# Two half-width score products, an earlier load of c, and a reordered end of layer 0 in a two-layer AdaLN kernel

## The chip, the cores and the metric

The kernel runs on one core of a Trainium2 chip. The core has a tensor engine (PE) with its own path for loading weights (PEld), a vector engine (DVE), a scalar engine (ACT), a general-purpose engine (POOL) and a sync engine (SP) that issues DMA transfers. Each engine works through its own queue in order and waits on semaphores for the others. The metric is the device time of one execution in microseconds (us); the median of three runs before the change is 2544.6 us (2543.75 to 2546.12).

## What is computed

Two transformer layers with adaptive layer norm, on x of 2 batches x 512 positions x 512 features, all in float32. Cut to what matters here:

```python
mod = (silu(L0_c) @ L0_wmod).reshape(2, 6, 1, -1)      # sa, ca, ga, sb, cb, gb
h = layernorm(x) * (1 + ca) + sa
# layer 0 attention: 32 query heads, 8 key/value heads, head size 128, window of 128
q, k, v = rope(h @ wq), rope(h @ wk), h @ wv
scores = q @ k.T * HEAD_DIM ** -0.5
allowed = (j <= i) & (j > i - 128)
x = x + ga * (softmax(where(allowed, scores, -inf)) @ v) @ wo
h = layernorm(x) * (1 + cb) + sb
# layer 0 feed-forward: one 512x512 product, a bias and 16 low-rank updates
x = x + gb * (h @ W.T + bias + sum_e coeffs[e] * scales[e] * (h @ A[e].T) @ Bf[e].T)
# layer 1: the same frame round latent attention with 128 heads and a routed low-rank FFN
```

The limit to ga and gb in size and the whole of layer 1 are left out; the change does not touch them.

## The kernel before

**Tiles.** A position block is 128 rows; each batch has TB = 4 of them. In layer 0 the attention is divided into 16 units, a unit being one key/value head (a "group" of 4 query heads) of one batch: units 0 and 1 are group 0 of batch 0 and 1, and so on. A unit has four blocks of queries, qb = 0 to 3. Because of the window of 128, a block of queries sees its own block of keys and the one before: 256 columns of scores, or 128 for qb = 0. A wide tile of scores is thus 128 queries x 4 heads x 256 keys (two PSUM banks), a narrow one 128 x 4 x 128.

**Steps.** `attention0` writes out the order of PE, DVE, ACT and POOL by hand (`manual_schedule`); SP is not in that order. It runs steps n = -4 to 65. With u, qb = divmod(n, 4), a step issues, in this order: `scores` of (u, qb); the keys, values or queries of the next unit (one `queries` a step, with `keys` at qb = 0 and `values` at qb = 1); `normalised` (the division by the row sum); `turned` of step n - 1 (transposes of the probabilities, `pt`, copied to `pT` by ACT for the first half of the keys and by DVE for the second); `output` of step n - 2 (`pw`, four products with wo, and the addition to x); `mix` of step n - 1 (`po`, the products with v, copied to `oT` by DVE); one item of `aside` while there are any (the modulation rows for later use, `psr` and what follows); and the extra items of `steps`. What is in `rest` follows after the last step. Since no unit follows unit 15, steps 60 to 63 have no keys, values or queries.

**Scores.** `scores` (L598) issues four products, one for each head, of 128 queries x nk keys, then on DVE the addition of the mask `band` (L610) and the negated row maximum `nm` (L616), then on ACT four exponentials with row sums (L620). The tile `s` is allocated anew in each step from a pool with one buffer. `band` is one 128 x 256 table with 0 where a query sees a key and -1e30 elsewhere.

**The start.** `silu_c` (L78) loads c of each layer (4 KB) through POOL's queue; ACT's exponential and DVE's three small operations (L84, L85, L88) make `sc`, the stationary operand of the modulation products `psr` (L103). SP loads the first two 1 MB pieces of wmod, the eight blocks of x, the rotary table, band, and the weights of group 0. SP may have eight loads open, and a later one waits for the landing of an earlier one. `Norm` computes the statistics of a block (`stats`, L171 and L172 on DVE), then for a batch the root on ACT and the normalised rows `xn` on DVE (`rows`, L179 to L184), then 16 transposes `pst` and the scaled, shifted copies `hT`, shared by ACT and DVE (`turn`). This part is ordered by the scheduler.

**The end of layer 0.** `finale` places the feed-forward's first parts among the last steps. `end` is 56, the first step of unit 14:

```python
for i in range(TB):
    steps[end + 2 + i] = [lambda i=i: n0.stats(i)]
    steps[end + 6 + i] = [lambda i=i: n0.stats(TB + i)]
steps[end + 4].insert(0, f.bias)
steps[end + 5].append(lambda: n0.rows(0))
steps[end + 6].insert(0, lambda: n0.turn(0, (0, 1), pool))
```

Block i of batch 0 gets its last addition in `output` of step end + 2 + i, the step at whose end its statistics stand; `rows(0)` (root and xn) stands at the end of step 61, the turning of batch 0 at the ends of 62 and 63, the low-rank products `low` (`psxa`) at the ends of 63 and 64. `tile(t)` is the feed-forward of one block (`psf`), and `add_bias` adds the gated bias to x. `f.bias` also loads the bias row, into a buffer of the attention's pool. The products named here (`pw`, `po`, `pst`, `psxa`, `psf`) share four PSUM buffers in rotation.

Of the kernel before, what the change touches and what calls it, by code (L numbers as in the profile page):

```python
# [25 lines left out]
NKV, GRP, HD, WIN = 8, 4, 128, 128  # L26

# [15 lines left out]
def adaln_kernel(ctx: ExitStack, tc: tile.TileContext, A: dict, out: bass.AP):  # L43
# [34 lines left out]
    def silu_c(L, pool):  # L78

        c = pool.tile([P, KC, B], F32, tag=f"c{L}", name=f"c{L}")  # L80
        nc.gpsimd.dma_start(out=c, in_=A[f"L{L}_cT"])
        e = pool.tile([P, KC, B], F32, tag=f"ce{L}", name=f"ce{L}")
        nc.scalar.activation(e, c, AF.Exp, scale=-1.0)
        nc.vector.tensor_scalar_add(e, e, 1.0)  # L84
        nc.vector.reciprocal(e, e)  # L85
        sc = pool.tile([P, KC, 32], F32, tag=f"sc{L}", name=f"sc{L}")
        nc.gpsimd.memset(sc, 0.0)
        nc.vector.tensor_mul(sc[:, :, :B], c, e)  # L88
        return sc
# [126 lines left out]
    class Ffn0:  # L216
# [6 lines left out]
        def loads(self):  # L223
# [13 lines left out]
            for i, n in enumerate(("L0_ffn_coeffs", "L0_ffn_scales")):  # L237
                for j in range(2):
                    src = A[n][j * 8 : (j + 1) * 8].unsqueeze(1).to_broadcast([8, R]).unsqueeze(2)
                    nc.sync.dma_start(out=co[:, i, j : j + 1], in_=src)  # L240
            self.wrow = self.mid.tile([P, 2], F32, tag="wrow", name="wrow0")
            nc.vector.tensor_mul(self.wrow, co[:, 0, :], co[:, 1, :])

        def bias(self):

            row = self.ap.tile([P, D], F32, tag="t1", name="biasrow0")
            nc.sync.dma_start(out=row, in_=A["L0_ffn_bias"].unsqueeze(0).to_broadcast([P, D]))
# [3 lines left out]
            for b in range(B):  # L251
                nc.gpsimd.tensor_mul(self.gb[b], row, self.gate[b])
# [38 lines left out]
    with ExitStack() as c01:  # L291
# [7 lines left out]
        with ExitStack() as c00:  # L299
# [34 lines left out]
            def finale(ap, pool):  # L334
# [5 lines left out]
                for i in range(TB):  # L340
                    steps[end + 2 + i] = [lambda i=i: n0.stats(i)]
                    steps[end + 6 + i] = [lambda i=i: n0.stats(TB + i)]
                steps[end + 4].insert(0, f.bias)
                steps[end + 5].append(lambda: n0.rows(0))
                steps[end + 6].insert(0, lambda: n0.turn(0, (0, 1), pool))
                steps[end + 7] = [
                    lambda: n0.turn(0, (2, 3), pool), lambda: f.add_bias(0), lambda: f.low(0, 0)
                ] + steps[end + 7]
                steps[end + 8].insert(0, lambda: f.low(0, 1))
                rest = [  # L350
                    lambda: n0.rows(1),
                    lambda: f.tile(0),
                    lambda: f.tile(1),
                    lambda: n0.turn(1, range(KC), pool),
                    lambda: f.add_bias(1),
                    lambda: f.tile(2),
# [8 lines left out]
                return steps, rest  # L365
# [129 lines left out]
def weights0(tc, A, ctx):  # L495
# [10 lines left out]
    def tables():  # L506
# [3 lines left out]
        band = tab.tile([P, 2 * P], F32, tag="band", name="band")  # L510
# [18 lines left out]
def attention0(tc, small, hT, xs, ga, ident, tabs, groups, load_group, aside, finale):  # L529
# [11 lines left out]
    with ExitStack() as ctx:  # L541
# [4 lines left out]
        kTs, vs, qTs, oTs, sps, pes, pTs = ({} for _ in range(7))  # L546
# [51 lines left out]
        def scores(u, qb):  # L598

            k0, nk = window(qb)  # L600
            sp = pss.tile([P, GRP, 2 * P], F32, tag="s", name=f"s{u}_{qb}")
            for hh in range(GRP):
                nc.tensor.matmul(  # L603
                    sp[:, hh, :nk],
                    lhsT=qTs[u][:, hh, qb * P : (qb + 1) * P],
                    rhs=kTs[u][:, k0 * P : k0 * P + nk],
                    start=True,
                    stop=True,
                )
            nc.vector.tensor_add(  # L610
                sp[:, :, :nk],
                sp[:, :, :nk],
                band[:, 2 * P - nk :].unsqueeze(1).to_broadcast([P, GRP, nk]),
            )
            nm = small.tile([P, GRP], F32, tag="nm", name=f"nm{u}_{qb}")
            nc.vector.tensor_reduce(nm, sp[:, :, :nk], AX.X, ALU.max, negate=True)  # L616
            pe = ap.tile([P, GRP, 2 * P], F32, tag="p", name=f"p{u}_{qb}", bufs=3)
            rs = small.tile([P, GRP], F32, tag="rs", name=f"rs{u}_{qb}")
            for hh in range(GRP):
                nc.scalar.activation(  # L620
                    pe[:, hh, :nk], sp[:, hh, :nk], AF.Exp,
# [54 lines left out]
        steps, rest = finale(ap, pmm)  # L676
        aside.pop(0)()
        with tc.manual_schedule(engines=FOUR):
            for n in range(-TB, NU * TB + 2):
# [20 lines left out]
                if 0 <= n - 2:  # L700
                    output(*last)
                if 0 <= n - 1 < NU * TB:
# [546 lines left out]
def _constants():  # L1249
# [12 lines left out]
    band = np.where((j > i) & (j <= i + WIN), 0.0, -1e30).astype(np.float32)  # L1262
# [71 lines left out]
```

## Time and profile before

| what | us |
|---|---|
| median of 3 runs | 2544.6 |
| the profiled execution | 2545.36 |
| its span on the core | 2543.6 |
| PE busy | 2454.6 |
| POOL busy | 1592.2 |
| DVE busy | 1672.9 |
| ACT busy | 1400.6 |
| L603, scores of layer 0, wide, busy | 91.3 |
| L603, scores of layer 0, narrow, busy | 18.0 |
| PE waiting at psr (L103) for sc (L88) | 13.3 |
| PE waiting at po (L650) for pT (L641) | 8.2 |

The span runs from the first instruction to the last. Busy time of PE is the union of its records; one product of the program in float32 makes two records. A record's length reaches past the start of the next one, because products are pipelined, so the cost of a block of products is read from the distance between starts, not from the lengths. The form "128*64" in a line of PE is the part of the array used, rows x columns. The mean clock granted to PE in this execution was 0.979 of full speed.

### The profile page before, as it was taken

How to read it: one execution, taken by the hardware profiler on the slowest of the kernel's cores; microseconds unless marked ns; L12 is line 12 of the kernel's file. 1: busy time of each engine (PE TensorE's matmuls, PEld its weight loads, DVE VectorE, ACT ScalarE, POOL GpSimd, SP SyncE). 2: the span in 40 equal slices, each digit the busy share in tenths (PEclk: the TensorE clock that was granted, in tenths of full speed). 3: DMA queues.
4: the chain of work that ended last, by engine and by line, in shares of the span. 5: the costliest groups of instructions: out<-in, count | busy, mean ns of one | idle time of the engine just before them, and what ended most of it. 6: DMA issues, size and time to landing. Idle time of an engine off the chain costs nothing.

```text
span 2543.6 us, 28531 instructions
## 1 busy us (share of the span) xinstructions
PE 2454.6 (97%) x10268; PEld 1148.9 (45%) x10268; DVE 1672.9 (66%) x2323; ACT 1400.6 (55%) x2083; POOL 1592.2 (63%) x1538
## 2 busy tenths in 40 slices
PE   7999999999999999999999999999999999999757
PEld 3555555555555444444444344444444434444233
DVE  4545555555555345788777778777878777887652
ACT  2112212212112215888888788878888878888710
POOL 1333333333333314888888888888888888888841
PEclk9999999999999999999999999999999999999868
DMA  6211101001000101000000000000000000000010
GB/s 233 85 51 64 42 5 38 26 20 38 17 1 7 29 15 33 26 19 24 26 26 26 30 19 25 26 26 26 30 18 26 26 26 25 24 23 17 1 32 33
DMA packets 68477, 81.31 MB, mean 32 GB/s; under 512 B 6865, under 2 KB 49520, under 8 KB 68208
## 3 DMA queue, kind: packets, MB, share of 16 engines
q1 hardware_dynamic: 67984, 79.21, 9.8%
q8 instruction: 81, 1.33, 0.2%
q14 instruction: 60, 0.49, 0.1%
q0 software_dynamic: 352, 0.28, 0.1%
HBM read 77.38 MB, written 2.10 MB: 31 GB/s over the span
## 4 chain that ended last, share of the span: by engine, by line
PE 93%; issue 2%; DVE 2%; POOL 2%; ACT 1%; DMA 0%; SPq 0%; POOLq 0%; DVEq 0%; ACTq 0%
PE s L948 18%; PE psq L881 18%; PE acc L1103 9%; PE ps_q L552 9%; PE pw L664 8%; PE s L957 5%; PE s L603 4%; PE po L650 4%; PE psv L574 2%; PE ps_k L552 2%; PE pt L639 2%; PE psu L900 2%; PE psm L1027 1%; PE psw L1159 1%; PE psf L275 1%
## 5 line engine op out<-in xcount | busy, mean ns | idle before, releaser
L1054 POOL TENSOR_TENSOR ss<-ss,row 128x512 f32<-128x512 f32 x512 | 644.6, 1287 | 39.3 <-ACT row L1039 39.3
L967 ACT COPY ss<-s 128x1024 f32<-128x1024 f32 x512 | 505.6, 1015 | 167.4 <-PE s L957 128.8
L948 PE MATMUL s<-q,ckr 64*128 64x512 f32 x2048 | 552.9, 611 | 7.6 <-ACT ss L967 7.6
L1057 ACT ACTIVATE ss<-ss 128x1024 f32<-128x1024 f32 x512 | 525.7, 1070 | 8.4 <-POOL ss L1048 4.0
L881 PE MATMUL psq<-hT,wqr 128*128 128x512 f32 x1024 | 466.7, 598 | 0.0
L957 PE MATMUL s<-qm,c 64*128 64x512 f32 x1024 | 417.9, 794 | 0.0
L620 ACT ACTIVATE p<-s,nm 128x256 f32<-128x256 f32 (+1 forms) x256 | 111.1, 446 | 488.0 <-DVE nm L616 479.2
L974 DVE TENSOR_TENSOR mx<-s,mx 128x1024 f32<-128x1024 f32 x256 | 306.5, 1218 | 41.1 <-PE s L957 40.1
L562 POOL TENSOR_TENSOR qT<-t_q,t_q 128x512 f32<-128x512 f32 x64 | 81.3, 1270 | 402.4 <-DVE t_q L561 402.4
L1048 POOL TENSOR_TENSOR ss<-ss,rowe 128x512 f32<-128x512 f32 x256 | 323.3, 1286 | 0.0
L881 PEld LDWEIGHTS psq<-hT,wqr 128*128 128x128 f32 x1024 | 189.0, 189 | 242.3 <-issue 211.7
L948 PEld LDWEIGHTS s<-q,ckr 64*128 64x128 f32 x2048 | 183.4, 186 | 212.7 <-ACT ss L967 97.2
L1103 PE MATMUL acc<-ss,vp 128*32 128x512 f32 x2048 | 265.7, 607 | 5.5 <-ACT ss L1057 5.5
L974 DVE TENSOR_TENSOR mx<-s,ss 128x1024 f32<-128x1024 f32 x128 | 156.8, 1225 | 117.5 <-ACT row L1039 78.0
L664 PE MATMUL pw<-wo,oT 128*128 128x512 f32 x512 | 230.3, 592 | 0.0
L552 PE MATMUL ps_q<-hT,wq 128*128 128x512 f32 x512 | 230.1, 592 | 0.0
L979 DVE STREAM_TRANSPOSE mx<-mx 128x1024 f32<-128x1024 f32 x128 | 158.6, 1239 | 2.2
L985 DVE TENSOR_REDUCE m<-mx 128x32 f32<-128x1024 f32 x128 | 156.2, 1220 | 4.4
L1050 DVE TENSOR_TENSOR ss<-ss,psm 128x512 f32<-128x512 f32 x256 | 158.0, 679 | 0.0
L957 PEld LDWEIGHTS s<-qm,c 64*128 64x128 f32 x1024 | 104.2, 187 | 117.7 <-issue 114.8
L1017 POOL TENSOR_TENSOR st<-mh,own_block 128x512 fp32r<-128x512 f32 x64 | 67.1, 1048 | 139.0 <-DVE mh L1013 139.0
L552 PEld LDWEIGHTS ps_q<-hT,wq 128*128 128x128 f32 x512 | 96.0, 190 | 102.4 <-issue 100.8
(193 smaller groups left out, 3089.3 us busy)
## 6 DMA issues: line engine op xcount, KB each, us to landing
wqr<-in_L_attn_Wq_rope_pairs SPq DMA_DIRECT2D x64, 512.0 KB
wmod<-in_L_wmod SPq DMA_DIRECT2D x12, 1024.0 KB
wq<-in_L_attn_wq SPq DMA_DIRECT2D x8, 1024.0 KB
wo<-in_L_attn_wo SPq DMA_DIRECT2D x8, 1024.0 KB
x<-in_L_attn_x SPq DMA_DIRECT2D x8, 256.0 KB
wk<-in_L_attn_wk SPq DMA_DIRECT2D x8, 256.0 KB
wv<-in_L_attn_wv SPq DMA_DIRECT2D x8, 256.0 KB
wT<-in_L_ffn_WT SPq DMA_DIRECT2D x2, 1024.0 KB
```

Source lines behind the costliest of these rows:

```text
L552: nc.tensor.matmul(ps, lhsT=wcols(kc), rhs=hT[b][:, kc, :], start=(kc == 0), stop=(kc == KC - 1))
L664: nc.tensor.matmul(ps, lhsT=oTs[u][:, hh, i * P : (i + 1) * P], rhs=groups[g]["o"][:, hh, :], start=(hh == 0), stop=(hh == GRP - 1),)
L881: nc.tensor.matmul(ps, lhsT=wqs[t][:, kc, pair * P : (pair + 1) * P], rhs=hT[b][:, kc, :], start=(kc == 0), stop=(kc == KC - 1),)
L948: nc.tensor.matmul(out[:, j, :], lhsT=whole[b]["kr"][r, bass.ts(i, P)], rhs=qs[t, p][r, :], start=True, stop=False,)
L957: nc.tensor.matmul(out[:, j, :], lhsT=qkc[t // 2, 1][r, bass.ts(i, P)], rhs=qm[t, p][r, :], start=False, stop=True,)
L967: nc.scalar.copy(ss[t, i, p], hold["s", t, i, p])
L974: nc.vector.tensor_max(mx[t, p], hold["s", t, i, p], before)
L979: nc.vector.transpose(m, m)
L1048: nc.gpsimd.tensor_sub(s, s, hold["r", t, 2])
L1054: nc.gpsimd.tensor_sub(s, s, hold["r", t, 2 * p + 1])
L1057: nc.scalar.activation(ss[t, i, p], ss[t, i, p], AF.Exp)
L1103: nc.tensor.matmul(accs[g, b][32 * h : 32 * (h + 1), :], lhsT=vps[t][:, kb, h, :], rhs=ss[t, kb, h // 2][:, h % 2, :], start=(s == 0 and k ...
```

## The change

There are three parts.

1. **Scores of wide tiles.** The tile of scores is allocated once, and filled once with -1e30 by DVE. In a wide tile each head's product is replaced by two: the first 64 queries against keys 0 to 191 of the 256, the last 64 against keys 64 to 255. They write the two halves of the PSUM partitions. The corners that no product writes (queries 0 to 63 with keys 192 to 255, queries 64 to 127 with keys 0 to 63) are always masked: they keep the large negative value, and the mask has 0 there. The narrow tile now lies in the last 128 columns. `band` grows to 128 x 384, with the narrow mask in its last third. DVE and ACT work on the same number of elements as before.
2. **c.** Its two loads are issued by SP instead of POOL, and stand first in SP's queue.
3. **The end of layer 0.** The statistics of a block stand one step later, `rows(0)` at the end of step 62, the statistics of the last block in `rest`. The turning of batch 0 (all four), the bias addition and `low(0, 0)` go into step 63 between `output` and `mix`, `low(0, 1)` likewise into step 64 (`filling`). In `rest`, `tile(2)` is ahead of the turning of batch 1. The bias row is loaded with the feed-forward's other weights into a buffer of its own.

The order of SP, which the scheduler makes, changes in the place of these loads: the two c first, and coefficients and bias row behind the third pair of wmod pieces, where the coefficients stood ahead of it. At the start, DVE's order now has the six operations for `sc` ahead of all statistics, and the two copies of the modulation columns (`mod`, L122) between the first `xn` and the other three.

```diff
-        nc.gpsimd.dma_start(out=c, in_=A[f"L{L}_cT"])
+        nc.sync.dma_start(out=c, in_=A[f"L{L}_cT"])
...
+            self.row = self.mid.tile([P, D], F32, tag="biasrow", name="biasrow0")
+            nc.sync.dma_start(out=self.row, in_=A["L0_ffn_bias"].unsqueeze(0).to_broadcast([P, D]))
...
-            row = self.ap.tile([P, D], F32, tag="t1", name="biasrow0")
-            nc.sync.dma_start(out=row, in_=A["L0_ffn_bias"].unsqueeze(0).to_broadcast([P, D]))
...
                 for i in range(TB):
-                    steps[end + 2 + i] = [lambda i=i: n0.stats(i)]
-                    steps[end + 6 + i] = [lambda i=i: n0.stats(TB + i)]
+                    steps[end + 3 + i] = [lambda i=i: n0.stats(i)]
+                for i in range(TB - 1):
+                    steps.setdefault(end + 7 + i, []).append(lambda i=i: n0.stats(TB + i))
                 steps[end + 4].insert(0, f.bias)
-                steps[end + 5].append(lambda: n0.rows(0))
-                steps[end + 6].insert(0, lambda: n0.turn(0, (0, 1), pool))
-                steps[end + 7] = [
-                    lambda: n0.turn(0, (2, 3), pool), lambda: f.add_bias(0), lambda: f.low(0, 0)
-                ] + steps[end + 7]
-                steps[end + 8].insert(0, lambda: f.low(0, 1))
+                steps[end + 6].insert(1, lambda: n0.rows(0))
+
+                filling = {
+                    end + 7: [
+                        lambda: n0.turn(0, (0, 1), pool), lambda: n0.turn(0, (2, 3), pool),
+                        lambda: f.add_bias(0), lambda: f.low(0, 0),
+                    ],
+                    end + 8: [lambda: f.low(0, 1)],
+                }
                 rest = [
+                    lambda: n0.stats(NT - 1),
                     lambda: n0.rows(1),
                     lambda: f.tile(0),
                     lambda: f.tile(1),
+                    lambda: f.tile(2),
                     lambda: n0.turn(1, range(KC), pool),
                     lambda: f.add_bias(1),
-                    lambda: f.tile(2),
                     lambda: f.tile(3),
...
+        sp = pss.tile([P, GRP, 2 * P], F32, tag="s", name="scores")
+        nc.vector.memset(sp, NEVER)
...
             k0, nk = window(qb)
-            sp = pss.tile([P, GRP, 2 * P], F32, tag="s", name=f"s{u}_{qb}")
-            for hh in range(GRP):
-                nc.tensor.matmul(
-                    sp[:, hh, :nk],
-                    lhsT=qTs[u][:, hh, qb * P : (qb + 1) * P],
-                    rhs=kTs[u][:, k0 * P : k0 * P + nk],
+            o = 2 * P - nk
+            for hh in range(GRP) if qb == 0 else ():
+                nc.tensor.matmul(
+                    sp[:, hh, o:],
+                    lhsT=qTs[u][:, hh, :P],
+                    rhs=kTs[u][:, :P],
                     start=True,
                     stop=True,
                 )
+            for hh in range(GRP) if qb else ():
+                for h in range(2):
+                    lo, hi = h * H2, 2 * P - (1 - h) * H2
+                    nc.tensor.matmul(
+                        sp[h * H2 : (h + 1) * H2, hh, lo:hi],
+                        lhsT=qTs[u][:, hh, qb * P + h * H2 : qb * P + (h + 1) * H2],
+                        rhs=kTs[u][:, k0 * P + lo : k0 * P + hi],
+                        start=True,
+                        stop=True,
+                    )
...
                 if 0 <= n - 2:
                     output(*last)
+                for f in filling.get(n, ()):
+                    f()
                 if 0 <= n - 1 < NU * TB:
                     mix(*before)
...
+    band = np.concatenate([band, band[:, P:]], axis=1)
+    band[:H2, 2 * P - H2 : 2 * P] = 0.0
+    band[H2:, :H2] = 0.0
```

## The prediction, made before the changed kernel ran

> **What bounds the kernel now.** I read the page's busy shares and chain of waits first, then the busy time by stretches, to see where TensorE (PE) ever waits.
>
> ```profile
> PE 2454.6 (97%) x10268; PEld 1148.9 (45%) x10268; DVE 1672.9 (66%) x2323; ACT 1400.6 (55%) x2083; POOL 1592.2 (63%) x1538
> PE 93%; issue 2%; DVE 2%; POOL 2%; ACT 1%; DMA 0%; SPq 0%; POOLq 0%; DVEq 0%; ACTq 0%
> 60.00:810.00 750.00, 749.32 (x2708) 421.10 (x2707) 404.95 (x577) 151.66 (x559) 263.55 (x192) 1.00 0.10 33
> ```
>
> The last line is a stretch: its bounds and length, busy us (instructions) of PE, PEld (weight loads), DVE, ACT and POOL, then granted clock, DMA share, GB/s. PE carries 93% of the chain, and from 60 to 810 us, nearly all of layer 0's attention, it is busy for 749.3 of 750.0 us. In that stretch a microsecond taken from PE is a microsecond of the kernel, and work moved between the other engines is worth nothing. Before 60 us and from 810 to 868 us PE waits; there the waits decide.
>
> Next, PE's own timeline. Columns: start, length, engine, line, operation; the distance between two starts is what a block costs.
>
> ```profile
> 107.93 3.60 PE L552 MATMUL ps_q<-hT,wq 128*128 128x512 f32 x8
> 111.37 1.04 PE L639 MATMUL pt<-ident,p 128*128 128x128 f32 x8
> ...
> 115.68 1.88 PE L650 MATMUL po<-pT,v 128*128 128x512 f32 x4
> 117.49 3.63 PE L103 MATMUL psr<-wmod,sc 128*32 128x512 f32 x16
> 121.04 1.99 PE L603 MATMUL s<-kT,qT 128*128 128x256 f32 x8
> 122.88 3.73 PE L574 MATMUL psv<-wv,hT 128*128 128x128 f32 x32
> 391.40 1.89 PE L603 MATMUL s<-kT,qT 128*128 128x256 f32 x8
> 393.13 3.60 PE L552 MATMUL ps_q<-hT,wq 128*128 128x512 f32 x8
> 117.94 0.12 PEld L103 LDWEIGHTS psr<-wmod,sc 128*32 128x32 f32 x2 [0.31 <-issue]
> ```
>
> A product of the program makes two records. ps_q: 8 records in 3.44 us, 0.43 each. A wide score tile (L603): 8 records in 1.73 us, 0.216 each. psr is the one block here that already uses column parts of the array (128*32): 16 records in 3.55 us, so two run at once, at 0.43 a pair.
>
> **Scores on column halves.** Each of 48 wide tiles (16 units x 3) gives up 8 records of 256 columns and gets 16 of 64x192, in 8 pairs if the halves run together. A record's price follows its columns (512: 0.43, 256: 0.216), so 192 cost 0.162 and the tile 8 x 0.162 = 1.30 us instead of 1.73: 0.43 saved.
>
> Against it stands the change of array shape, which psr shows: po's four records should take 4 x 0.43 = 1.72 and psr starts after 1.81 (+0.09); psr should take 3.43 and lasts 3.55 (+0.12); the tile behind it lasts 1.84 instead of 1.73 (+0.11). Together 0.32 us. The 0.11 is the uncovered load of 128 columns, the first load of 32 columns is about 0.03 of the 0.12; 64 columns make that about 0.05. So one excursion costs 0.35 and a tile 1.65: **0.08 us saved**. Three wide tiles stand directly behind psr, where part of this is paid already (about 0.2 each).
>
> The Trainium skill has a rule against this ("TensorE: Matmul & The Clock Gate", Part 3, "The mechanism"): a weight load overlaps matmuls in flight only when its row group differs. Both halves use all 128 rows, so by the rule each pair would wait for its loads. psv shows loads at their limit: 32 of 128 columns in 3.57 us, 0.112 each, 0.056 for 64; 8 x 0.056 = 0.45 us a tile, 2.10 in all, 48 x 0.37 = 18 us *lost*. The row says otherwise: psr's loads run at 117.94, beside its matmuls, and its pairs keep ps_q's 0.43. I take the row. What it doesn't show is 64-column loads under a pair of only 0.162; a load record lasts 0.12 for 32 columns and 0.19 for 128, so I expect about 0.14, still covered, with little to spare.
>
> Sum: 45 tiles in the PE-bound part x 0.076 = 3.4, and 3 x 0.2 = 0.6: **-4.0 us** (ends: an excursion of 0.32 gives -5.4, one of 0.42 gives -0.9). DVE's mask and maximum and ACT's exponentials keep their sizes. The one filling of the scores bank with the mask value, a DVE operation on 128x1024 (the nearest row, the mask's addition at L610, takes 1.23), falls into the 1.34 us that DVE idles ahead of its first t_q at 31.4: nothing, and behind it some 20 us until s needs the keys. No new wait: the one tile for scores is still freed by the exponentials of a step before, some 6 us earlier.
>
> **c first.** The start, from the timelines of DVE, PE and SP and SP's waits:
>
> ```profile
> 12.05 0.66 DVE L171 BATCH_NORM_STATS2 bn<-x 128x6 f32<-128x512 f32 x1
> 12.63 0.23 DVE L84 TENSOR_SCALAR ce<-ce 128x8 f32<-128x8 f32 x2
> 13.34 6.11 PE L103 MATMUL psr<-wmod,sc 128*32 128x512 f32 x16 [13.34 <-DVE sc L88]
> 20.16 0.46 PE L119 MATMUL psm<-ident,rows 64*128 64x64 f32 x4 [0.71 <-ACT rows L111]
> 8.94 0.33 SPq L57 DMA_DIRECT2D x<-in_L_attn_x  x1
> SPq L57 <- DMA wmod<-in_L_wmod: 3.2, 2, 2.5
> ```
>
> SP's last issue of x, at 8.94, waited for the second wmod: both were there then, but psr began at 13.34, since DVE took c's six small operations only behind the statistics of x0 to x3. Now they come first, and c (4 KB a copy) lands long before x. The price: two more issues at the head of SP's queue. The first two wmod issues take 0.99 us there, so everything behind lands 0.85 later, wmod at 9.8. psr: 9.8 to 15.9 at its length of 6.1 (the clock is granted only during it: 5.1 to 6.8). rows, psm and the two mod follow by 17.4. Here a gain is given back: in the changed order DVE has the two mod *between* the first xn and the other three, so these (0.48 each) end at 18.9, where before all four were done at 17.25 and waited for mod until 20.9. Transposes, hT and the second batch's xn follow: the last xn at about 24.0 instead of 25.1, and through ps_k's remaining pieces ps_q starts at 27.05 instead of 27.78: **-0.7 us** (+0.5 to -1.5). From there PE's waits are as before.
>
> The bias row's DMA now goes out with the coefficients, on SP behind the third pair of wmod, hundreds of us before they are needed: nothing. The 128 KB band grows by 64 KB; issued at 10.3, first used at 59.0. POOL is rid of c's two issues (0.74 and 0.56 us); it idles there.
>
> **The end of layer 0.** Steps n = 60 to 65, no queries left to cover:
>
> ```profile
> 824.72 1.12 PE L650 MATMUL po<-pT,v 128*128 128x512 f32 x2 [1.24 <-ACT pT L641]
> 837.36 3.77 PE L650 MATMUL po<-pT,v 128*128 128x512 f32 x4 [5.48 <-ACT pT L641]
> 840.94 1.06 PE L193 MATMUL pst<-ident,xn 128*128 128x128 f32 x8
> 829.19 1.92 DVE L184 TENSOR_SCALAR xn<-x,mv,rstd 128x512 f32<-128x512 f32 x4
> 831.02 1.23 DVE L610 TENSOR_TENSOR s<-s,band 128x1024 f32<-128x1024 f32 x1
> 833.61 1.28 ACT L620 ACT_TABLE_LOAD   x1 [4.66 <-DVE nm L616]
> ```
>
> po waits 1.24, 5.48 and 0.80 us for pT, whose copy stands on ACT behind the step's four exponentials, which follow mask and maximum on DVE. The long wait is step 62: statistics, root and four xn hold back its mask to 831.02, and the table load adds 1.28.
>
> I replayed the changed queues from here with these rows' durations (0.2 us from a product to its reader; the same reckoning of the old order gives waits of 1.39, 5.76 and 0.95). Step 62 loses its burden: po starts at 832.4 after 0.95. Step 63 gets it. Its s ends at 835.6, its mask waits for statistics, root and xn to about 838.3, the exponentials and table load end near 844. PE has pt, pw and the twelve transposes of pst 0 to 2 until 841.4. The fourth pst needs the buffer of the pw four allocations back, freed by ya on DVE, and that now stands behind the reciprocal that waits for the exponentials: 845.7. The two hT on ACT stand behind them too, so psxa cannot start before 846.1. **A new wait of 4.35 us**, then 0.96 at the last pw, because low(0,1) no longer covers po's copy. Waits 7.7 against 8.1 by the same reckoning; with the shorter tiles (0.15) the first psf comes 0.6 us earlier.
>
> The clock matters too: po at 837.36 takes 3.6 us for four records that take 1.72 elsewhere, 1.9 lost. The Trainium skill (the same page, Part 1, "What's actually happening") lets the clock fall after a window of about 3.4 us that is idle; a wait of 4.35 holds a whole such window in some 3 of 10 cases, so by the rule 1.3 us more would be saved. But here the stretches show it at 0.50 from 52.5 on too, after a wait of 2.11 us only. By that row 4.35 costs about the same 1.9: **-0.6 us** (+1 to -2.5). The third psf moved ahead of the transposes of batch 1 covers nothing, since PE has no wait there.
>
> **Sum.** The profiled execution took 2545.4 us (span 2543.6 and 1.8 around it): -4.0 - 0.7 - 0.6 = -5.3, 2540.1. The median shown is 0.8 lower than that execution, so **2539.3 us**, -0.21%. What the measurement can tell from no change is 0.2%, 5.1 us: below 2539.5 is faster, above 2549.7 slower.
>
> **Rivals.**
> 1. *The loads are not hidden at 192 columns.* Slower, one mechanism in the pair of halves: gain and loss cross where a pair costs 0.172 instead of 0.162. If a 64-column load stays outside each pair it is the 18 us worked out above: about 2561. For it: the rule, and the slot is little longer than a load. Against: psr's pace. If the halves take turns altogether, 16 x 0.162 + 0.35 - 1.73 = 1.2 a tile, about 2601; psr speaks plainly against that. Together 0.15.
> 2. *A dearer change of shape*: at 0.42 an excursion the tiles give 0.9 in all, the sum is -2.2, 2542.4: no measurable difference. For it: no row shows 64-column parts. Against: the entry of 0.09 recurs at psx to s in layer 1 with 64-row parts. 0.09.
> 3. *More at both ends*: a clock kept at the end (-1.9) and psr granted its clock early (-0.8): 2536.6. For it: where the clock's windows fall is chance. Against: the short wait at 51 us that sufficed. 0.15.
> The forecast itself has 0.61, cut by the 5.1 us bound nearly in half: 0.38 faster, 0.23 same.
>
> Faster 0.38 + 0.15 = 0.53; same 0.23 + 0.09 = 0.32; slower 0.15. Range 2534 to 2546: forecast and rivals 2 and 3 with the ends of their unknowns (about 0.85).
>
> **What would show it.** In the changed trace a wide tile is 16 records, starts in pairs a few ns apart and 0.16 us between pairs, with 1.65 us to the block behind. Pairs at 0.21 or more, or singly, make it wrong on the slow side. psr should start near 9.8 and ps_q near 27.0; if psr's start is still near 13, c was not what it waited for. At the end, po of step 61 should wait about 1 us, and the long wait, about 4.4 us, stand at the fourth pst. A first psf later than its old distance from the last s would make that part a loss.

## The result and the profile after

The changed kernel takes **2537.41 us** (2535.17 to 2539.42) against 2544.6 us: a ratio of 0.9970, 95% interval 0.9957 to 0.9983. That is 7.2 us less; the prediction said 5.3 less, 2539.3. The profiled execution took 2539.42 us (span 2537.6), 5.9 less than the profiled one of before. Both medians are now of seven runs each, one of which on either side was far off (3943.76 us at a granted clock of 0.594, and 3641.28 us before); without it the medians are 2536.55 and 2544.18, 7.6 us apart, and the ratio and its interval are of these. A later comparison of the same two kernels gave 2537.71 against 2544.97 us, 0.9971 (0.9960 to 0.9983).

The spans of the two profiled executions are cut here at three landmarks on PE's timeline. A second trace of the changed kernel, taken with the later comparison, stands beside them. The landmarks of before are these rows (those of after stand further down):

```profile
27.78 3.60 PE L552 MATMUL ps_q<-hT,wq 128*128 128x512 f32 x8
...
810.75 1.05 PE L603 MATMUL s<-kT,qT 128*128 128x128 f32 x8
...
867.86 3.60 PE L275 MATMUL psf<-wT,hT 128*128 128x512 f32 x8
```

| stretch | before | after | difference | after, second trace |
|---|---|---|---|---|
| start to the first ps_q | 27.78 | 26.56 | -1.22 | 25.98 |
| to the narrow scores of the last unit | 782.97 | 778.26 | -4.71 | 779.96 |
| to the first psf | 57.11 | 55.82 | -1.29 | 56.85 |
| to the end of the span | 1675.7 | 1677.0 | +1.2 | 1673.2 |
| span | 2543.6 | 2537.6 | -6.0 | 2536.0 |

The last stretch holds of the change only the order of a few feed-forward parts, and it differs by 3.8 us between two traces of one kernel. So single traces can be compared stretch by stretch, but their sums are good to a few us only.

In the second stretch the clock must be alike for a comparison. PE's granted clock is 0.50 there from 52.51 to 59.33 us before and from 52.02 to 58.85 after, 6.8 us in both, but from 50.52 to 60.76 in the second trace, 10.2 us: 3.4 us more at half clock are the 1.70 by which its 779.96 is longer. From unit 1 to unit 15, behind that place, both traces of after take the same time to 0.01 us (703.07 and 703.06).

The page of the changed kernel, busy times and engine shares of the chain that ended last:

```profile
PE 2453.6 (97%) x10652; PEld 1124.8 (44%) x10652; DVE 1673.9 (66%) x2324; ACT 1400.1 (55%) x2083; POOL 1590.8 (63%) x1536
...
PE 92%; DVE 3%; issue 2%; POOL 1%; ACT 1%; DMA 0%; POOLq 0%; SPq 0%; DVEq 0%; ACTq 0%
```

There are 384 more records on PE (48 tiles by 8), and the busy sum is only 1 us lower. The sum is no measure of the saving: in the first 60 us PE's busy time rises from 43.84 to 47.86, since psr takes 7.87 us instead of 6.11 (four of its 16 records now start singly, at 7.055, 7.878, 14.638 and 15.068, where all 16 started in pairs before), and more of what follows falls ahead of the cut. The stretch that PE fills, in the busy times by stretches (the same columns as in the prediction):

```profile
60.00:805.00 745.00, 744.33 (x3068) 397.16 (x3067) 403.64 (x574) 150.25 (x558) 264.43 (x193) 1.00 0.10 33
```

It is as full as before and at full clock; it is cut at the last unit's narrow scores, which come 5.9 us earlier. So what the tiles save arrives whole at the end of this stretch.

**A steady tile**, on PE's timeline (start, length, engine, line, operation):

```profile
386.65 1.02 PE L672 MATMUL po<-pT,v 128*128 128x512 f32 x2
387.61 1.52 PE L625 MATMUL scores<-kT,qT 128*64 128x192 f32 x16
389.06 3.70 PE L563 MATMUL ps_q<-hT,wq 128*128 128x512 f32 x8
```

Two records of po take 0.95 instead of 0.86, the tile 1.45, and the ps_q behind it 3.54 instead of 3.43 up to the next block: 1.65 for the tile with its excursion to another array shape and back, against 1.73. The starts of single records, from the same trace, in us:

```
387.607 387.613 | 387.820 387.827 | 387.982 387.989 | 388.145 388.152
388.307 388.314 | 388.470 388.477 | 388.632 388.639 | 388.795 388.802 | ps_q 389.057
```

Pairs 7 ns apart, one pair every 0.162 us. The operations on that tile (ns: least, median, most):

```profile
L625 PEld LDWEIGHTS scores<-kT,qT x16: 133/137/137, 387.6 to 388.6; 128*64 128x64 f32 x16
L625 PE MATMUL scores<-kT,qT x16: 326/326/377, 387.6 to 388.8; 128*64 128x192 f32 x16
```

A load of 64 columns lasts 0.137, and two of them per pair still hide. At the changes of shape the first load does not: it starts together with its product, at 387.605 for the first scores record and at 389.056 for ps_q, where in the trace of before ps_q's first load starts 0.21 us ahead of its product (392.915 and 393.129).

**The start**, PE's timeline, DVE's, and SP's queue:

```profile
7.05 1.88 PE L105 MATMUL psr<-wmod,sc 128*32 128x512 f32 x2 [7.05 <-DMA wmod<-in_L_wmod]
9.67 5.99 PE L105 MATMUL psr<-wmod,sc 128*32 128x512 f32 x14 [0.73 <-DMA wmod<-in_L_wmod]
16.33 0.46 PE L121 MATMUL psm<-ident,rows 64*128 64x64 f32 x4 [0.67 <-ACT rows L113]
...
26.56 1.88 PE L563 MATMUL ps_q<-hT,wq 128*128 128x512 f32 x4
```

```profile
3.62 0.30 DVE L90 TENSOR_TENSOR sc<-c,ce 128x8 f32<-128x8 f32 x2
10.34 0.69 DVE L173 BATCH_NORM_STATS2 bn<-x 128x6 f32<-128x512 f32 x1 [6.42 <-DMA x<-in_L_attn_x]
...
15.94 0.53 DVE L186 TENSOR_SCALAR xn<-x,mv,rstd 128x512 f32<-128x512 f32 x1
16.82 0.24 DVE L124 TENSOR_SCALAR mod<-psm 128x8 f32<-128x8 f32 x2 [0.36 <-PE psm L121]
16.98 1.45 DVE L186 TENSOR_SCALAR xn<-x,mv,rstd 128x512 f32<-128x512 f32 x3
```

```profile
0.74 0.87 SPq L83 DMA_DIRECT2D c<-in_L_cT  x2
1.65 0.98 SPq L75 DMA_DIRECT2D wmod<-in_L_wmod  x2
2.68 7.29 SPq L59 DMA_DIRECT2D x<-in_L_attn_x  x8
```

psr no longer waits for sc, which is ready at 3.9, but for wmod itself. The first statistics (bn) move from 9.63 to 10.34 us: that is the price of the two issues in front.

**The end of layer 0**, PE's timeline of steps 60 to 65:

```profile
804.82 1.05 PE L615 MATMUL scores<-kT,qT 128*128 128x128 f32 x8
...
818.53 1.12 PE L672 MATMUL po<-pT,v 128*128 128x512 f32 x2 [1.09 <-ACT pT L663]
...
826.23 1.98 PE L672 MATMUL po<-pT,v 128*128 128x512 f32 x4 [0.66 <-ACT pT L663]
...
839.18 0.66 PE L195 MATMUL pst<-ident,xn 128*128 128x128 f32 x4 [3.75 <-ACT hT L205]
839.67 5.29 PE L264 MATMUL psxa<-hT,abT 128*128 128x512 f32 x8
...
857.10 3.70 PE L686 MATMUL pw<-wo,oT 128*128 128x512 f32 x8 [0.78 <-DVE oT L679]
860.64 3.60 PE L277 MATMUL psf<-wT,hT 128*128 128x512 f32 x8
```

The 5.48 us wait of po, which the prediction shows, is gone; a new one of 3.75 stands at the fourth pst, and 0.78 at the last pw. Four waits of 6.28 us replace three of 7.52. What released the fourth pst (pst 3) is on ACT's timeline:

```profile
834.74 1.28 ACT L642 ACT_TABLE_LOAD   x1 [4.65 <-DVE nm L638]
...
837.85 0.60 ACT L663 COPY pT<-pt 128x512 f32<-128x512 f32 x1
838.32 1.48 ACT L205 ACTIVATE hT<-pst,mod,mod 128x512 f32<-128x512 f32 x2
```

Two hT of 0.81 us each; the first, the reader of pst 0, ends at 839.13, and 0.05 later PE writes pst 3. The multiplication ya on DVE, which frees the buffer of pw, ends only at 839.36, so it is not what pst 3 waited for: the four buffers are not handed out in plain rotation.

### The profile page after: what moved, and what is told of

Read it like the earlier page. It is cut to its first block, busy times and chain, and to the rows that moved or that the text cites. A ratio compares the mean times of both kernels' runs of the same rounds, so it can differ in the third digit from the quotient of the medians.

```text
span 2537.6 us, 29270 instructions
## 1 busy us (share of the span) xinstructions
PE 2453.6 (97%) x10652; PEld 1124.8 (44%) x10652; DVE 1673.9 (66%) x2324; ACT 1400.1 (55%) x2083; POOL 1590.8 (63%) x1536
## 4 chain that ended last, share of the span: by engine, by line
PE 92%; DVE 3%; issue 2%; POOL 1%; ACT 1%; DMA 0%; POOLq 0%; SPq 0%; DVEq 0%; ACTq 0%
PE s L972 18%; PE psq L905 18%; PE acc L1127 9%; PE ps_q L563 9%; PE pw L686 8%; PE s L981 5%; PE po L672 4%; PE scores L625 3%; PE psv L585 2%; PE ps_k L563 2%; PE pt L661 2%; PE psu L924 2%; PE psm L1051 1%; PE psw L1183 1%; PE psf L277 1%
## 5 line engine op out<-in xcount | busy, mean ns | idle before, releaser
L642 ACT ACTIVATE p<-scores,nm 128x256 f32<-128x256 f32 (+1 forms) x256 | 111.1, 446 | 482.1 <-DVE nm L638 473.1
```

## The experiments

Times are medians beside runs of the kernel before on the same chip. The experiments ask which part gives what, and why the halves run together.

### 1. Whole tiles again

```diff
-            for hh in range(GRP) if qb == 0 else ():
+            for hh in range(GRP):
...
-            for hh in range(GRP) if qb else ():
-                for h in range(2):
...
```

The changed kernel with the wide tiles of before.

> The changed kernel with its wide tiles of scores as whole products again (4 of 128 x 256; full mask in band). My theory: a wide tile on halves costs 1.65 us with its two changes of array shape, a whole one 1.73, and three tiles behind psr save 0.2 more, so this run is 4.0 us slower than the changed kernel (about 2541.4, ratio to before 0.9987), and the distance on PE from the first ps_q to the narrow scores of unit 15 grows from 778.3 to about 782.3 us (the clock's share at psg aside). Rival: the changed kernel gained at the start and the end alone and the halves are worth nothing: 2537.4, and the distance stays at 778.

2543.28 us (2542.63 to 2545.21), ratio 0.9994 (0.9985 to 1.0003). The time of four steps of steady work (one unit) returns to 49.62 us, the figure of before; in the changed kernel it is 49.39. From unit 1 to unit 15 that is 707.14 against 703.07 us. The rest of the change is worth 1.7 us here, too little for the times to tell from nothing. The kernel is 1.9 us above the expectation: the scores are worth more than the 4.0 that it put on them.

### 2. The scores alone

The kernel before with the column halves, the mask and the one scores tile, c and the end as before.

> The kernel before with part 1 alone (scores of wide tiles on halves). My theory: -4.0 us against before, about 2540.6 (ratio 0.9984), start and end as before: first ps_q at 27.8, first psf about 57 us behind the narrow scores of unit 15. Rival (halves worth nothing): 2544.6.

2539.28 us (2537.21 to 2541.42), ratio 0.9976 (0.9967 to 0.9985); from unit 1 to unit 15 it takes 703.06 us. Most of the gain is the scores, by both ways of asking: 5.7 us added alone, 5.9 taken away.

### 3. Halves that do not alternate

```diff
-            for hh in range(GRP) if qb else ():
-                for h in range(2):
+            for h in range(2) if qb else ():
+                for hh in range(GRP):
```

The same 16 records, all first halves ahead of all second ones.

> The changed kernel with the order of a wide tile's eight products turned: first the four of queries 0 to 63, then the four of queries 64 to 127, so that neighbours in the queue use the same column half. My theory: products start in the order of the queue and two run at once only when neighbours use different halves, so the records stand singly at 0.16 us, a tile costs 16 x 0.162 + 0.35 = 2.94 us, 48 x 1.29 = 62 us more: about 2599. Rival: PE pairs products out of its queue whatever their order[...]: 2537, records still in pairs.

2571.41 us, ratio 1.0102 (1.0088 to 1.0116): 34 us over the changed kernel, and neither expectation. A tile on PE's timeline:

```profile
400.92 2.22 PE L625 MATMUL scores<-kT,qT 128*64 128x192 f32 x16
403.07 1.98 PE L563 MATMUL ps_q<-hT,wq 128*128 128x512 f32 x4
```

2.15 us, between 1.45 (all in pairs) and about 2.7 (one by one). The record starts fall into two streams of eight at 0.162:

```
400.924 401.137 401.300 401.463 401.625 401.788 401.950 402.113
                                401.631 401.845 402.006 402.170 402.332 402.494 402.656 402.819
```

The records do not say which half they belong to; they are put into streams here by the 0.162 between two starts, which is what one record of 192 columns costs. Read so, the second stream begins when the fifth record of the first has just started, ahead of three that stand before it in the program. So PE does start a product for the other column half past waiting ones, but only so far. Halves must be issued close to each other to pair throughout. 48 tiles by 0.70 us are the 34.

### 4. The narrow tiles on halves too

```diff
-                nc.tensor.matmul(
-                    sp[:, hh, o:],
-                    lhsT=qTs[u][:, hh, :P],
...
+                for h in range(2):
+                    nc.tensor.matmul(
+                        sp[h * H2 : (h + 1) * H2, hh, o:],
+                        lhsT=qTs[u][:, hh, h * H2 : (h + 1) * H2],
```

No columns are saved here, so it leaves the price of an excursion, and it tests the loads at a shorter pair.

> The changed kernel with the 16 narrow tiles on halves too (each of 64 queries x 128 keys, no column left out), so nothing is saved and the pairs are shorter than a load record of 0.14 us. My theory: loads are pipelined as in the full array (0.19 us of load record at a pace of 0.112), a pair costs 0.11, a narrow tile grows by the change of shape alone: 16 x 0.35 = 5.6 us more than the changed kernel, about 2543. Rival: a pair cannot be shorter than its load: 0.137 a pair, 8 x 0.137 + 0.35 - 0.89 = 0.56 a tile, 9 us more, about 2546.5. With loads outside the pair (the rule weighed in the prediction): over 0.16 a pair, 12 us or more.

2543.0 us (2541.74 to 2544.84), ratio 0.9992 (0.9983 to 1.0001), 5.6 above the changed kernel, as the theory had it.

```profile
411.28 1.09 PE L616 MATMUL scores<-kT,qT 128*64 128x128 f32 x16
412.31 3.70 PE L563 MATMUL ps_k<-hT,wk 128*128 128x512 f32 x8
```

1.02 us where the whole tile takes 0.89, and 0.10 more on either side. Pairs start every 0.109 us (411.441, 411.551, 411.660), which is shorter than one load record of 0.137: loads overlap matmuls and each other.

### 5. c first, alone

```diff
-        nc.gpsimd.dma_start(out=c, in_=A[f"L{L}_cT"])
+        nc.sync.dma_start(out=c, in_=A[f"L{L}_cT"])
```

> The kernel before, with nothing changed but the queue of c's two loads: SP, ahead of everything, instead of POOL. Theory (c's late softmax-like steps on VectorE held psr back, as in the changed kernel): psr's first pair starts as soon as the first block of wmod has landed, near 7, the rest near 9.7, and the first ps_q comes at 26.6 to 27.2 us instead of 27.78. The time falls by about 1 us against the kernel before, ratio 0.9996. Rival (the two more issues at the head of SP's queue delay x and the later weights by 0.85 us and cancel the gain): first ps_q at 27.7 or later, no fall or a rise by up to 0.5 us. In both cases the steady unit step stays at 49.62 us.

2542.8 us (2539.72 to 2544.76), ratio 0.9993 (0.9985 to 1.0002). The time alone does not decide; PE's timeline does:

```profile
9.62 5.45 PE L103 MATMUL psr<-wmod,sc 128*32 128x512 f32 x14 [0.73 <-DMA wmod<-in_L_wmod]
...
25.91 2.31 PE L552 MATMUL ps_q<-hT,wq 128*128 128x512 f32 x5
```

Over all traces of the study: the first ps_q comes at 27.32 to 27.78 us (mean 27.55, three traces) with c on POOL and at 25.91 to 26.86 (mean 26.35, eight traces) with c at the head of SP. The gain is 1.2 us. Much of the spread within a group is psr's own length: its 14 records take 5.45 us here, 5.99 and 5.30 in the two traces of the changed kernel.

### 6. The end alone

The kernel before with part 3 of the change only.

> The kernel before with the change at the end of layer 0 alone (statistics and root one step later, transposes of xn and the low products put between output and mix). Scores and c as before. Theory (the long wait moves from po of step 61, 5.5 us, to the fourth pst, and comes back shorter, because other work now stands ahead of it): po of step 61 waits about 1 us, the fourth pst 3.5 to 4.5 us, and the stretch from the last unit's narrow scores to the first psf falls from 57.1 to about 56.2 us; the time falls by 0.6 to 1.3 us against the kernel before, ratio 0.9996. Rival (the wait only changes its place, and the gain in the changed kernel at this end, 1.3 us, came from the shorter score tiles and the clock): stretch at 56.9 to 57.3 us, and no fall.

2545.23 us (2542.38 to 2546.28), ratio 1.0000 (0.9991 to 1.0009): no difference that the times show, and not the fall of 0.6 to 1.3 us that was expected.

```profile
811.99 1.05 PE L608 MATMUL s<-kT,qT 128*128 128x128 f32 x8
...
846.89 1.01 PE L193 MATMUL pst<-ident,xn 128*128 128x128 f32 x4 [3.63 <-ACT hT L203]
847.70 4.97 PE L262 MATMUL psxa<-hT,abT 128*128 128x512 f32 x8
```

The stretch to the first psf is 56.35 instead of 57.11 us and its waits sum to 6.45 instead of 7.52, as expected. In the same trace the clock is at 0.50 from 51.74 to 61.98 us, 3.4 us longer than before; this costs 1.70 us ahead of unit 1 and hides the gain at the end in this execution's time. Added alone, the three parts give -5.7, -1.6 and +0.8 us by their times, -6.5 together, against -7.2 for the whole: they add up within what the times can tell.

### 7. c on ScalarE's queue

```diff
-        nc.sync.dma_start(out=c, in_=A[f"L{L}_cT"])
+        nc.scalar.dma_start(out=c, in_=A[f"L{L}_cT"])
```

> The changed kernel with c's two loads issued by ScalarE instead of SP; nothing else is different. It measures the price of the two issues at the head of SP's queue (0.87 us for the pair). Theory (wmod and x land that much later because of them, and psr, mod and the normalised x follow the second wmod): psr's second part starts near 8.8 instead of 9.67, the first ps_q comes at 25.7 to 26.0 us instead of 26.56, and the time is 0.6 to 0.9 us below the changed kernel's, about 2536.7. Rival (the start is set by the landing of x or by the clock, which is granted at the same moment in both): ps_q within 0.2 us of 26.56, no fall.

2536.23 us (2534.41 to 2539.84), ratio 0.9971 (0.9959 to 0.9983).

```profile
7.10 6.21 PE L105 MATMUL psr<-wmod,sc 128*32 128x512 f32 x16 [7.10 <-DVE sc L90]
...
25.72 2.74 PE L563 MATMUL ps_q<-hT,wq 128*128 128x512 f32 x6
```

psr now runs through without its second wait, the first statistics stand at 9.49 instead of 10.34, and ps_q comes at 25.72 (25.24 to 25.72, mean 25.45, in three kernels with this edit). The two issues on SP cost the start 0.9 us (26.35 against 25.45), as reckoned. psr begins no earlier, since sc comes at 7.1 by this way. By the intervals the time is not told apart from the changed kernel's.

### 8. pst 3 behind the mix

```diff
+                steps[end + 7][:0] = [lambda: n0.turn(0, (3,), pool), lambda: f.low(0, 0)]
+                steps[end + 8].insert(0, lambda: f.low(0, 1))
...
-                        lambda: n0.turn(0, (0, 1), pool), lambda: n0.turn(0, (2, 3), pool),
-                        lambda: f.add_bias(0), lambda: f.low(0, 0),
+                        lambda: n0.turn(0, (0, 1, 2), pool), lambda: f.add_bias(0),
...
-                    end + 8: [lambda: f.low(0, 1)],
```

> The changed kernel with the fourth transpose block of the first batch (pst 3) and the two low products of that batch placed one step later, behind the mix of their step: so that po of step 62 stands ahead of the wait, and low(0,1) lies ahead of the last pw again. Theory (the 3.75 us wait of the fourth pst is dead time that po and mix can fill, and the last pw's wait of 0.78 us is covered by low(0,1) as in the kernel before): the stretch from the last unit's narrow scores to the first psf falls from 55.8 to about 54.3 us, and the time is about 1.5 us below the changed kernel's, near 2536. Rival (po of step 62 waits for the same exponentials as the fourth pst, so that the wait only changes its name; and psxa comes later): stretch at 55.5 us or more, no fall.

2535.02 us (2533.73 to 2537.25), ratio 0.9964 (0.9951 to 0.9976).

```profile
838.97 2.61 PE L672 MATMUL po<-pT,v 128*128 128x512 f32 x4 [3.76 <-ACT hT L205]
841.37 1.06 PE L195 MATMUL pst<-ident,xn 128*128 128x128 f32 x4
...
859.24 3.60 PE L277 MATMUL psf<-wT,hT 128*128 128x512 f32 x8
```

Half right. The stretch falls to 54.63 us, 1.19 less, but po does not fill the wait: it takes the wait over, 3.76 for 3.75, released by the same hT. I read it so that whatever product stands next needs a buffer, and all are held until ACT gets to hT; a fifth buffer, which would show it, was not tried. What went is mostly the 0.78 at the last pw, and 0.29 at three slower blocks (pw takes 3.44 and 3.43 instead of 3.54 twice, pt 0.87 instead of 0.95). By the intervals the time is not told apart from the changed kernel's.

### 9. Four column parts

```diff
-                for h in range(2):
-                    lo, hi = h * H2, 2 * P - (1 - h) * H2
+                for h in range(4):
+                    lo, hi = h * H4, P + (h + 1) * H4
...
-                        sp[h * H2 : (h + 1) * H2, hh, lo:hi],
-                        lhsT=qTs[u][:, hh, qb * P + h * H2 : qb * P + (h + 1) * H2],
+                        sp[h * H4 : (h + 1) * H4, hh, lo:hi],
+                        lhsT=qTs[u][:, hh, qb * P + h * H4 : qb * P + (h + 1) * H4],
...
-    band[:H2, 2 * P - H2 : 2 * P] = 0.0
-    band[H2:, :H2] = 0.0
+    for h in range(4):
+        band[h * H4 : (h + 1) * H4, P + (h + 1) * H4 : 2 * P] = 0.0
+        band[h * H4 : (h + 1) * H4, : h * H4] = 0.0
```

> The changed kernel with each wide score tile on four column parts of 32 queries and 160 columns of keys instead of two of 64 and 192 (the mask's always-hidden rectangles cut to match). It asks how far the two halves' running side by side goes. Theory A (four parts run at once, a load of 32 columns stays hidden): 4 groups of four at 0.135 us, 0.54, and an excursion of 0.35, make a tile of 0.89 instead of 1.65; 45 tiles by 0.76 = 34 us, about 2503, unit step 47.1. Theory B (all four run at once but the weight loads, 0.055 us for each as the narrow halves allowed at most, set the pace): 16 x 0.055 + 0.35 = 1.23, 19 us, about 2518, unit step 48.1. Rival C (two at a time, whatever the number of parts): 8 x 0.135 + 0.35 = 1.43, 10 us, about 2527, unit step 48.7. Rival D (one at a time): 16 x 0.135 + 0.35 = 2.51, 39 us slower than the changed kernel, about 2576, unit step 52.

**2527.45 us** (2525.91 to 2531.04), ratio 0.9932 (0.9918 to 0.9945), unit step 48.71: the number of rival C. But the records say theory A:

```profile
395.34 1.29 PE L625 MATMUL scores<-kT,qT 128*32 128x160 f32 x32
396.56 3.70 PE L563 MATMUL ps_q<-hT,wq 128*128 128x512 f32 x8
```

```profile
L625 PEld LDWEIGHTS scores<-kT,qT x32: 106/110/110, 384.5 to 385.3; 128*32 128x32 f32 x32
L625 PE MATMUL scores<-kT,qT x32: 299/299/323, 384.5 to 385.5; 128*32 128x160 f32 x32
```

32 records, in groups of four that start 7 ns apart (384.754, .761, .768, .774), a group every 0.136 us. All four parts run at once, with loads hidden. My expectation counted one record for a product where the program makes two, so A's own figure should have been 8 x 0.135 + 0.35 = 1.43, the figure given for C; without the record starts the right number would have stood for the wrong mechanism. A tile costs 0.23 us less than on halves, 45 of them 10.2, and the times differ by 10.3 (against the 2537.71 of the changed kernel beside it).

### 10 to 12. Both ends together, the changed kernel again, and all of it

> The changed kernel with both of the two last runs' edits: c's loads issued by ScalarE, and pst 3 with the low products of the first batch behind the mix. Theory: the two act in different stages and add up, first ps_q at 25.7, and 54.6 us from the last unit's narrow scores to the first psf (up to 0.8 more if the slow interval of the clock falls badly); the time about 2 us below the changed kernel's, near 2535. Rival (they aren't independent, since the earlier start moves where the clock's intervals fall at the end): no gain over either alone, 2536 or more.

2537.92 us (2532.63 to 2540.55), ratio 0.9967 (0.9954 to 0.9979), beside 2537.71 for the changed kernel on the same chip: no gain. Its trace has the first ps_q at 25.38 and 54.65 us to the first psf, as the theory wants. Both edits do what they should in the trace, and the median does not show it. The five runs fall into two groups: 2532.63 and 2533.57 us at a mean granted clock of 0.981 and 0.980, and 2537.92 to 2540.55 at 0.977 and 0.978; the changed kernel's six beside them had 0.980 to 0.982. A thousandth of the clock over 2537 us is 2.5 us of full clock, so the lower clock covers what the three slower runs lack. Where in the kernel they lost it is open, since the one trace is of the run of 2533.57.

> The changed kernel itself once more, beside the two runs above on the same chip, for a second trace of it. Where the granted clock's slow intervals fall should differ, the rest repeat: unit step 49.39, tile 1.65; first ps_q 26.2 to 26.9; the last unit's narrow scores to the first psf 55.7 to 56.6; the time 2536 to 2539.

2537.71 us (2536.94 to 2538.67). The time and the unit step (49.39) came as expected, the first ps_q (25.98) a little too early and the stretch to the first psf (56.85) too long. The waits of the end repeat to 0.02 us, but not its length:

```profile
840.31 1.12 PE L195 MATMUL pst<-ident,xn 128*128 128x128 f32 x4 [3.77 <-ACT hT L205]
841.22 5.89 PE L264 MATMUL psxa<-hT,abT 128*128 128x512 f32 x8
```

pst and psxa behind the long wait take 6.64 us to the next block, against 5.63 in the first trace and 3.88 at full clock. PE resumes at 839.18 in the first trace, where the granted clock is 0.50 from 840.50 to 843.92, and at 840.31 in the second, where it is 0.50 from 839.00 to 845.83. So one and the same wait costs 1.75 or 2.76 us more by the clock that follows it.

> The kernel on four column parts together with c's loads on ScalarE and pst 3 behind the mix. Theory (three stages, each bound by itself): unit step 48.71, first ps_q 25.4 to 25.7, the wait at the end filled as before; about 2 us below the kernel on four parts alone, near 2525.5. Rival (the clock's intervals at both ends take it back, as the time of the last combined run suggests): 2527 or more.

2526.74 us (2518.49 to 2530.02), ratio 0.9929 (0.9916 to 0.9941): between theory and rival, and not told apart from four parts alone. These two are the fastest kernels here.

## Why the prediction came out right, step by step

**Scores: right in kind and price.** Pair 0.162, excursion 0.35 and tile 1.65 were all met: the entry was put at 0.09 and measured 0.10, the tile's own length over 8 pairs was put at 0.15 and measured 1.45 - 1.30, the product behind was put at 0.11 and measured 0.10. Two rows of the trace of before had the price: ps_q's records by their columns, and psr, the one block already on column parts. The sum of 4.0 was small because of a count: it had three tiles behind other array shapes at 0.2. There are six, three behind psr and three behind psm. One behind psm, in the trace of before:

```profile
91.93 0.46 PE L119 MATMUL psm<-ident,rows 64*128 64x64 f32 x4
92.32 1.99 PE L603 MATMUL s<-kT,qT 128*128 128x256 f32 x8
94.15 3.60 PE L552 MATMUL ps_q<-hT,wq 128*128 128x512 f32 x8
```

Such a tile took 1.83 and takes 1.45, with 0.10 more at the product behind: 0.28 saved each. 39 x 0.077 + 6 x 0.28 = 4.7 for the 45 tiles ahead of the last unit's narrow scores; the two profiled executions, alike in clock there, have 4.71.

**The rivals on the scores fell.** The Trainium skill's rule on row groups ("TensorE: Matmul & The Clock Gate", Part 3, "The mechanism") would have put each pair's loads outside, 18 us lost. Pairs of 0.162 and 0.109 us and groups of 0.136 us, all on the same 128 rows and with loads of 0.106 to 0.138 us, disagree: for products on different columns the rule does not hold here. The same section lets a load go ahead into a background weight buffer too, which the prediction left out, and the trace of before has that overlap even on the whole array: the load for the first record of s starts at 390.975, beside a record of po that starts at 390.973. Nor could psv price a load, as the prediction had it: its records also move 128 columns, and at ps_q's price per column these alone take 0.108 of the 0.112. Halves that start singly exist, but only for another order of issue and in part (run 3). The dearer excursion (0.42) was not there.

**c first: right mechanism, gain mis-sized.** Predicted 27.05, measured 26.56 and 25.98, and -1.2 over the eleven traces with c on POOL or SP, instead of -0.7. The term that was off is psr: I let all of it wait for the second wmod (9.8), but its first two records run at 7.05, behind the first wmod. The other 14 start at 9.67 and 9.55 and take 5.99 and 5.30 instead of 6.1, so psr is done at 15.66 and 14.86 instead of 15.9. That is 0.24 and 1.04 of the 0.49 and 1.07 us by which ps_q came ahead of the reckoning; the rest of the first trace's lies behind psr and was not traced further. How much is due to the two early records, and how much to the moment from which psr's pairs start 0.43 instead of 0.85 us apart, the runs do not separate. The delay of x (0.85 by the reckoning, 0.71 measured) and the mod between the first and the other xn were there as put.

**The end: right place, wrong releaser.** po of step 61 waits 0.66 (said 0.95), the fourth pst 3.75 (4.35), the last pw 0.78 (0.96). The prediction gave the fourth pst the buffer that ya on DVE frees; it was the one that hT on ACT frees. Both stand behind the same exponentials (hT ends at 839.13, ya at 839.36), so it was luck that the number survived the mistake; run 8, built on moving PE's order, met the buffers instead. The waits fall by 1.24 where the replay gave 0.4. The end's order alone takes 0.65 us off the stretch (run 6: 0.76, of which 0.11 is a smaller loss to the clock), the shorter tiles 0.50 (run 2: 56.39 us, 0.72 less, of which 0.22 is the clock) instead of 0.15. Together 1.15. The first trace of after shows 1.29 and the second only 0.26; with the clock's loss taken out (1.86 before, 1.75 and 2.76 after) they show 1.18 and 1.16.

**The clock.** The row (a loss of 1.9) was taken against the skill's rule of a whole idle window (Part 1 of the same page, "What's actually happening": 1.3 less on average). Measured losses are 1.75 and 2.76, so the row was the better guide, and what it could not give was the spread. Rival 3 (2536.6) is nearer to the measured 2537.4 than the forecast: its quicker start came in part, its other half, a clock kept at the end, in no trace here.

**The sum.** With each term as the runs size it, 4.7 for the tiles, 1.2 for the start and 1.15 for the end make about 7.1, against 7.2 by the medians and 7.6 by the fast ones; the prediction had 4.0, 0.7 and 0.6. That the sum meets the medians so closely is partly luck, since the last stretch alone moves by 3.8 us between two traces. All three terms were too small, the first two by a count and a start time that the trace of before already showed in part (psm ahead of s; the first wmod landing on its own), the third by the replay, which gave too little to the waits and to the shorter tiles.

## What to carry to other kernels

Where a product's result is banded or triangular, split the stationary operand by columns into parts that each see only their own range, and issue the parts of one head next to each other; price it by columns per record plus about 0.35 us for each excursion to another array shape and back, and put such tiles next to work that already has another shape (0.28 us saved there, 0.08 elsewhere). Read the start times of single records, not the total, to see whether parts run together. Moving a product out of a wait in PE's order can hand the wait to the next product, as in run 8: look first whether a buffer is what is missing.

## What the runs showed of the hardware

- Products on different columns of the array overlap even when they share all 128 rows: two at a time on halves, four on quarters, 7 ns apart, with weight loads of 0.137 us hidden down to a pair every 0.109 us (run 4).
- PE starts a product for free columns past three records still waiting in the program's order (run 3), so PE's starts are not strictly in the order of its queue. This is read from the spacing of the starts, and that it is the limit of PE's reach from one pattern only.
- At a change of array shape the first weight load starts together with its product instead of 0.21 us ahead of it (ps_q, starts at 389.056 and 389.057), and a block gets longer: by 0.10 us on the way in and 0.10 on the way back at the steady tile.
- After the same wait of 3.75 us PE lost 1.75 us in one trace and 2.76 us in another, as the clock stayed at 0.50 for 3.4 or 6.8 us. For work at the scale of 0.1%, that is as large as the edits themselves.
